# Two attention layers in one kernel: the first pair of the second layer scaled into other memory, its first biases added later, and the last two rows and the stored reciprocals handled in another order

## The chip, the cores and the metric

The kernel runs on one core of a Trainium2 chip. A core has TensorE (PE, with its weight loads shown apart as PEld), VectorE (DVE), ScalarE (ACT), GpSimd (POOL) and SyncE (SP), which here issues most DMAs. Each engine takes its instructions in the order in which the program wrote them, and waits on semaphores for what others produce. The metric is the device time of one execution in microseconds; lower is better.

## The reference

The input x has 128 rows of 256 positions with 256 channels. Two layers follow, each a residual attention over a group-normalised input:

```python
x = x + L0_conv_ref(_gn(x), ...)   # 8 heads, pair bias from z, mask, gate
x = x + L1_conv_ref(_gn(x), w_in, b_in, w_out, b_out, 16)

def L1_conv_ref(x, w_in, b_in, w_out, b_out, band):   # 4 heads, 64 channels each
    qkv = x @ w_in.T + b_in
    q, k, v = heads of the three thirds
    scores = q @ k.T / sqrt(64)
    keep = |i - j| <= band
    attn = softmax(where(keep, scores, -inf))
    return (attn @ v) @ w_out.T + b_out
```

The attention runs within a row of 256 positions. The group norm of layer 1 takes its means and variances over the whole output of layer 0, so layer 1 can't scale its first row before the last row of layer 0 is known.

## The kernel before, in words

All arithmetic is float32. Rows are handled in pairs: NP = 64 pairs of two rows. Layer 0 writes its output rows from the tile `xo` to a DRAM array `x1` (the trace calls it x), eight rows per store. Its weights wq, wk, wv and wg stay in tiles of 128 x 512 for the whole program.

**Between the layers.** The last pair's data for layer 1's pair 0 were loaded and turned early: they lie transposed in wq and wk. `norm1` works out a scale `R1c` and an offset `nM1` per channel, while TensorE runs products without use (L1882, called `busy`)[...]. `centre(k)` (L1948) then scales one half of a pair's transposed channels on ACT into the tile `xgT`, tag xgT, which has two buffers in a pool that lies where layer 0 had its tiles. Pair 0 is projected directly (`project`, `values`); from pair 1 on the projections use a scheme of seven products for eight (`product`, `join`), whose input differences `differences` computes on POOL. Pair 1 is loaded from `x1` by SP (L1930), transposed by DVE (`turn`, L1943) and scaled by ACT. `add_bias` (L1954) adds b_out on POOL to a pair's residual rows `xt`.

**The pair loop of layer 1** is written out by hand, one pass per pair p. `now` is pair p, `was` p-1, `old` p-2, `nxt` p+1, `nn` p+2, `n3` p+3. In each pass `now.scores` makes the scores of both rows, takes their exponentials on ACT and multiplies them by the band mask on POOL (L2063); `was.apply(1)` and `now.apply(0)` multiply by the values (L2077) and sum the weights (L2085); `nxt` is projected; `copy_sums`, `join_sums`, `invert` (L2108) and `weigh` (L2113) normalise; `was.out_product` makes the output projection; `old.keep_rows` adds the residual rows on POOL and stores.

**Range tests.** A kernel for general inputs stands behind this one. Whether it must run is decided at the end from the tile `ok`: `look` puts two entries on a queue, one reduction for the largest value, and a comparison with a reduction for the smallest (L2223, L2220, L2221, all on DVE). `some_checks(n)` takes n entries, from the queue `late` if it has any, else from `checks`. The reciprocals of the softmax sums of layer 1 are tested in two ways: those of the first 56 pairs are stored to the DRAM array `rsum1`, loaded again in pass 58 as one block of 128 x 896 and put on `checks`; those of the last LATE = 8 pairs are put on `late` straight from the tile. From pass 57 on a pass makes four late entries and takes four.

**The end.** After the loop come the rows of pair 62 (`out_row`), then those of pair 63: `out_block` makes the products on TensorE (L2133), all remaining entries run on DVE, `okmin` (L2389) is their least value, and `keep_row` (L2193) adds the residual on DVE and stores a row (L2201). A product with `ones` (L2394) counts the partitions that are in range, DVE writes `verdict` (L2396), every engine loads it, and branches (L2407) past the general kernel.

Of the kernel before, what the change touches and what calls it, by code (L numbers as in the profile page):

```python
# [9 lines left out]
F32 = mybir.dt.float32  # L10
AF = mybir.ActivationFunctionType
# [5 lines left out]
P = 128  # L17
# [756 lines left out]
def fast_kernel(  # L774
# [25 lines left out]
    nc = tc.nc  # L800
    S, I, C = x.shape
# [6 lines left out]
    NB = I // P  # L808
    KC = C // P
    NP = S // 2  # L810
    N2 = 2 * I
# [97 lines left out]
    def rows(ap, s0, n):  # L909
        return ap[s0 : s0 + n].rearrange("s (b p) c -> p (s b) c", p=P)  # L910
# [933 lines left out]
    LATE = 8  # L1844
    rsum1 = dram.tile([NP, H1, 2, I], F32, name="rsum1")
    with tc.tile_pool(name="l1", bufs=2) as sb, tc.tile_pool(
# [5 lines left out]
        def mm1(name, side=0):  # L1852
            return ps_s.tile([P, 512], F32, name=name, tag=f"s{side}")
# [67 lines left out]
        class Pair1:  # L1921
# [21 lines left out]
                nc.vector.transpose(self.xT.rearrange("p k n -> p (k n)"), self.xs.rearrange("p k n -> p (k n)"))  # L1943

            def centre(self, k):
                if k == 0:
                    self.xgT = sb.tile([P, KC, N2], F32, name="xgT1", tag="xgT")
                nc.scalar.activation(  # L1948
                    self.xgT[:, k, :], self.xT[:, k, :] if self.p else self.xT[k], AF.Identity,
                    bias=nM1[:, k : k + 1], scale=R1c[:, k : k + 1],  # L1950
                )

# [3 lines left out]
            def differences(self):  # L1956

                self.dT = sb.tile([P, 4, I], F32, name="dT1", tag="dT")
                b = [[self.xgT[:, k, r * I : (r + 1) * I] for r in range(2)] for k in range(KC)]
                t1, t2, t3, t4 = (self.dT[:, n] for n in range(4))  # L1960
                nc.gpsimd.tensor_tensor(t1, b[0][1], b[0][0], ALU.subtract)
                nc.gpsimd.tensor_tensor(t2, b[1][1], t1, ALU.subtract)
                nc.gpsimd.tensor_tensor(t3, b[1][1], b[0][1], ALU.subtract)
                nc.gpsimd.tensor_tensor(t4, b[1][0], t2, ALU.subtract)
# [10 lines left out]
            def product(self, n, i):  # L1975

                if len(self.ps) == n:
                    self.ps.append([mm1("ps_qk", n % 2) for _ in range(2)])
                    self.u.append(sm.tile([P, 3, I], F32, name="u1", tag=f"u{n}", bufs=1))
                x, y = (ps[:, :I] for ps in self.ps[n])  # L1980
                w = lambda m, k: w_in[:, k, n * C + m * P : n * C + (m + 1) * P]
                b = lambda k, r: self.xgT[:, k, r * I : (r + 1) * I]
                to, lhs, rhs, start = {
                    1: (x, w(0, 0), b(0, 0), True),
                    2: (y, w(0, 1), b(1, 0), True),
                    6: (x, wst[:, 1, n], self.dT[:, 1], False),
                    5: (y, wst[:, 0, n], self.dT[:, 0], True),
                    7: (x, wst[:, 2, n], self.dT[:, 2], False),
                    4: (x, w(1, 1), self.dT[:, 3], False),
                    3: (y, wst[:, 3, n], b(1, 1), False),  # L1990
                }[i]
                if n == 2:
                    for b in range(NB):
                        at = slice(b * P, (b + 1) * P)
                        nc.tensor.matmul(  # L1995
                            to[:, at], rhs[:, at], lhs, start=start and b == 0, stop=True, skip_group_check=True
                        )
                else:
                    nc.tensor.matmul(to, lhs, rhs, start=start, stop=True, skip_group_check=True)  # L1999
                u = self.u[n]  # L2000
                if i in (2, 5, 3):
                    return
                at = (1, 6, 7, 4).index(i)
                to = self.to[n](1, 0) if i == 4 else u[:, at]
                if n == 2:
                    nc.scalar.copy(to, x.rearrange("p (b c) -> p b c", b=NB) if i == 4 else x)
                else:
                    nc.scalar.activation(to, x, AF.Identity, bias=bin_c[:, n * KC + (at > 1) : n * KC + (at > 1) + 1])  # L2008
# [8 lines left out]
            def project(self, which, m):  # L2017
                n = ("qT", "kT").index(which)
                if m == 0:
                    setattr(self, which, sb.tile([P, KC, N2], F32, name=f"{which}1", tag=which))  # L2020
                ps = mm1("ps_p1", m)
                for k in range(KC):
                    nc.tensor.matmul(
                        ps, w_in[:, k, n * C + m * P : n * C + (m + 1) * P], self.xgT[:, k, :],
                        start=(k == 0), stop=(k == KC - 1),
                    )
                nc.scalar.activation(
                    getattr(self, which)[:, m, :], ps, AF.Identity, bias=bin_c[:, n * KC + m : n * KC + m + 1]
                )

            def values(self, r, side=0):
                if r == 0:
                    self.v = sb.tile([P, 2, NB, C], F32, name="v1", tag="v")
                ps = mm1("ps_v1", side)
                for b in range(NB):
                    t = r * NB + b
                    for k in range(KC):
                        nc.tensor.matmul(
                            ps[:, b * C : (b + 1) * C], self.xgT[:, k, t * P : (t + 1) * P], w_in[:, k, 2 * C : 3 * C],
                            start=(k == 0), stop=(k == KC - 1),  # L2040
                        )
                nc.scalar.copy(self.v[:, r, :, :].rearrange("p b c -> p (b c)"), ps)
# [142 lines left out]
            def keep_rows(self):  # L2185
                nc.gpsimd.tensor_tensor(self.yo, self.yo, self.xt, ALU.add)
                nc.sync.dma_start(rows(out, 2 * self.p, 2), self.yo)

            def keep_row(self, r):
                if r == 0:  # L2190
                    self.yo = sb.tile([P, 2 * NB, C], F32, name="yo", tag="yo")
                if self.p == NP - 1:
                    nc.vector.tensor_tensor(  # L2193
                        self.yo[:, r * NB : (r + 1) * NB, :], self.whole.rearrange("p (b c) -> p b c", b=NB),
                        self.xt[:, r * NB : (r + 1) * NB, :], ALU.add,
                    )
                for t in range(r * NB, (r + 1) * NB if self.p < NP - 1 else 0):
                    nc.vector.tensor_tensor(self.yo[:, t, :], self.y[t - r * NB], self.xt[:, t, :], ALU.add)
                s0 = 2 * self.p
                if self.p == NP - 1:  # L2200
                    nc.sync.dma_start(rows(out, s0 + r, 1), self.yo[:, r * NB : (r + 1) * NB, :])  # L2201
                elif r == 1:
                    nc.sync.dma_start(rows(out, s0, 2), self.yo)
# [34 lines left out]
        def load_sums(src, name):  # L2238
            t = sb.tile([P, src.shape[0] // P], F32, name=name, tag=name, bufs=1)
            nc.sync.dma_start(t, src.rearrange("(a b) -> a b", a=P))  # L2240
            look_all(t, 1e-16)

        with tc.manual_schedule():
# [9 lines left out]
            for m in range(KC):  # L2253
                now.project("qT", m)
                now.project("kT", m)
                nxt.centre(m)
            nxt.differences()
            for r in range(2):
                now.values(r)
            now.add_bias()  # L2260
            nxt.add_bias()
            look_all(eb.rearrange("p h b i -> p (h b i)"), math.exp(-20.0))
            n_eb = cols[0]

# [1 line left out]
            for p in range(NP - 1):  # L2266
# [4 lines left out]
                if p == 1:  # L2271
                    mask_t = sb.tile([S, I], F32, name="mask_all", bufs=1)
                    nc.sync.dma_start(mask_t, mask)
                    look_all(mask_t, 1e-15)
                    n_mask = cols[0]
                    load_sums(rsum.rearrange("n q r c i -> (n q r c i)"), "sums0")
                if p == NP - LATE + 2:
                    load_sums(rsum1[: NP - LATE].rearrange("n q r i -> (n q r i)"), "sums1")

                now.scores(0)  # L2280
                now.scores(1)
                old.keep_rows()
                was.apply(1)
                nxt.begin_fast()
# [92 lines left out]
            now.apply(1)  # L2377
            now.copy_sums(1)
            now.copy_odd(1)
            for b in range(NB):  # L2380
                now.out_block(0, b)
            now.join_sums(1)
            now.invert(1)
            now.join_odd(1)
# [2 lines left out]
            below(n_mask, cols[0], 1e8)  # L2387
            tot = sm.tile([P, 1], F32, name="okmin", bufs=1)
            nc.vector.tensor_reduce(tot, ok.rearrange("p a n -> p (a n)"), AX.X, ALU.min)  # L2389
            now.keep_row(0)  # L2390
            for b in range(NB):
                now.out_block(1, b)
            ps = mm1("ok_ps")
            nc.tensor.matmul(ps[:, 0:1], ones, tot, start=True, stop=True)  # L2394
            now.keep_row(1)
        nc.vector.tensor_scalar(verdict, ps[0:1, 0:1], P - 0.5, None, ALU.is_lt)  # L2396


# [63 lines left out]
```

## Time and profile before

| | |
|---|---|
| time, median of 3 runs | 3098.26 us (3097.44 to 3100.63) |
| time of the profiled execution | 3098.43 us |
| its span | 3096.7 us |
| mean granted TensorE clock | 0.987 |
| first scaling of layer 1 (L1948) | 1980.06 us |
| first pass that starts at the loop's usual distance (L2052) | 2026.3 us |
| start of the verdict (L2396) | 3089.94 us |

Lines of the timeline give the start, the duration, the engine, the source line, the operation, its output and inputs, and in brackets how long the engine had been idle and what released it. The chain of waits is followed back from the last instruction; its lines give the start, the length and what held the time. A line of the clock by stretches gives the stretch, its length, the busy time of PE, PEld, DVE, ACT and POOL with the number of instructions, the mean granted TensorE clock, the DMA share and GB/s.

### The profile page before, as it was taken

The page shows a single profiled execution, that of the slowest core. Times are in us where ns is not written, and L with a number is a line of the kernel's source. Part 1 is how long each engine was busy: PE and PEld are TensorE (multiplying, and loading weights), DVE is VectorE, ACT ScalarE, POOL GpSimd, SP SyncE. Part 2 cuts the span into 40 slices and gives each one's busy share as a digit, 9 for nine tenths or more (in the row PEclk, how much of TensorE's full clock was granted, in tenths as well). Part 3 has the DMA queues.
Part 4 walks back from the last instruction along what each step waited for, and adds up shares of the span by engine and source line. Part 5 has one row for each costly group of instructions (what it writes and reads, how often), then busy time and mean ns, then how long its engine had stood idle before and what let it go on. Part 6 is the DMA issues. An engine that isn't in the chain of part 4 may idle for free.

```text
span 3096.7 us, 83063 instructions
## 1 busy us (share of the span) xinstructions
PE 2991.3 (97%) x34386; PEld 2088.0 (67%) x34386; DVE 2374.1 (77%) x4075; ACT 1656.8 (54%) x2887; POOL 2587.0 (84%) x1950
## 2 busy tenths in 40 slices
PE   6689999999999999999999999899999999999998
PEld 4355555665555655555655555588888888888886
DVE  7987677777777777777777777688887877777787
ACT  3454544444444444444444444366666666666664
POOL 3469899898898888898888898588888888888885
PEclk9799999999999999999999999999999999999999
DMA  9952333323333332333333233433434343434341
GB/s 357 390 190 53 100 70 100 95 65 93 100 97 73 96 90 67 100 97 91 78 89 95 73 97 87 112 89 93 99 90 104 86 105 85 105 92 97 94 100 44
DMA packets 690787, 328.06 MB, mean 106 GB/s; under 512 B 538624, under 2 KB 639872, under 8 KB 689248
## 3 DMA queue, kind: packets, MB, share of 16 engines
q1 hardware_dynamic: 686000, 320.02, 38.8%
q8 instruction: 273, 4.47, 0.6%
q10 hardware_dynamic: 4400, 2.63, 0.3%
q14 instruction: 114, 0.93, 0.1%
HBM read 253.83 MB, written 68.74 MB: 104 GB/s over the span
## 4 chain that ended last, share of the span: by engine, by line
PE 89%; DVE 4%; DMA 4%; POOL 1%; issue 1%; ACT 1%; SPq 0%; ACTq 0%; POOLq 0%; DVEq 0%
PE ps_p L1364 21%; PE ps_qk L1999 12%; PE ps_sc L1401 9%; PE ps_ov L1436 8%; PE ps_v L1382 7%; PE ps_y L1490 7%; PE ps_su_y L2170 6%; PE ps_qk L1995 6%; PE ps_o L2077 4%; PE ps_su L1444 3%; PE ps_sc L2052 3%; PE ps_su_y L2085 2%; DMA xa<-in_x_dram 2%; DMA zt<-in_z_dram 1%; DVE st L1199 1%
## 5 line engine op out<-in xcount | busy, mean ns | idle before, releaser
L1425 POOL TENSOR_TENSOR eboth<-e 128x512 f32<-128x512 f32 x512 | 744.2, 1475 | 174.2 <-PE ps_su L1444 95.2
L1421 DVE TENSOR_TENSOR e<-ps_sc,eb 128x1024 f32<-128x1024 f32 x384 | 458.2, 1221 | 288.7 <-ACT ps_sc L1413 288.6
L1413 ACT ACTIVATE ps_sc<-ps_sc 128x1024 f32<-128x1024 f32 x384 | 375.4, 1007 | 435.8 <-PE ps_sc L1401 310.0
L2063 POOL TENSOR_TENSOR e<-e,bw 128x384 f32<-128x384 f32 x256 | 276.6, 1111 | 77.4 <-ACT e L2061 77.4
L1401 PE MATMUL ps_sc<-qT,kT 32*128 32x256 f32 x4096 | 293.9, 400 | 0.0
L1401 PEld LDWEIGHTS ps_sc<-qT,kT 32*128 32x128 f32 x4096 | 185.5, 184 | 101.5 <-issue 91.5
L1490 PEld LDWEIGHTS ps_y<-wo,oT 128*128 128x128 f32 x1024 | 194.2, 190 | 81.8 <-issue 44.0
L1436 PE MATMUL ps_ov<-e,v 128*32 128x256 f32 x4096 | 247.6, 382 | 1.1 <-DVE v L1388 1.1
L1364 PE MATMUL ps_p<-xnT,wq 128*128 128x512 f32 x512 | 247.5, 605 | 0.1
L1364 PE MATMUL ps_p<-xgT,wg 128*128 128x512 f32 x512 | 247.3, 605 | 0.0
L1490 PE MATMUL ps_y<-wo,oT 128*128 128x256 f32 x1024 | 242.0, 379 | 1.7 <-POOL oT L1480 1.7
L1382 PE MATMUL ps_v<-wv,xnT 128*128 128x256 f32 x1024 | 241.8, 379 | 0.0
L1364 PE MATMUL ps_p<-xnT,wk 128*128 128x512 f32 x512 | 240.7, 592 | 0.0
L1382 PEld LDWEIGHTS ps_v<-wv,xnT 128*128 128x128 f32 x1024 | 194.5, 190 | 54.0 <-issue 30.9
L2008 ACT ACTIVATE u<-ps_qk,bin_c 128x256 f32<-128x256 f32 x378 | 174.7, 477 | 93.0 <-PE ps_qk L1999 93.0
L2108 DVE RECIPROCAL rv<-sums 128x256 f32<-128x256 f32 x128 | 223.0, 1742 | 0.0
L1436 PEld LDWEIGHTS ps_ov<-e,v 128*32 128x32 f32 x4096 | 120.0, 109 | 109.4 <-issue 41.5
L1116 POOL TENSOR_TENSOR zrs<-zrs,mhalf 128x32 f32<-128x32 f32 (+1 forms) x19 | 87.9, 4631 | 114.4 <-DVE zrs L1109 114.4
L1371 ACT ACTIVATE gT<-ps_p,bg_c 128x512 f32<-128x512 f32 x128 | 87.9, 687 | 175.1 <-PE ps_p L1364 175.1
L1364 PEld LDWEIGHTS ps_p<-xnT,wk 128*128 128x128 f32 x512 | 97.2, 190 | 122.8 <-issue 122.6
L1999 PE MATMUL ps_qk<-dT,wst 128*128 128x256 f32 x756 | 173.5, 379 | 0.0
L1364 PEld LDWEIGHTS ps_p<-xnT,wq 128*128 128x128 f32 x512 | 91.9, 189 | 114.0 <-issue 112.0
(254 smaller groups left out, 7061.1 us busy)
## 6 DMA issues: line engine op xcount, KB each, us to landing
xa<-in_x_dram SPq DMA_DIRECT2D x8, 4096.0 KB
xt<-in_x_dram SPq DMA_DIRECT2D x64, 512.0 KB
x<-xo SPq DMA_DIRECT2D x16, 2048.0 KB
xt<-x SPq DMA_DIRECT2D x64, 512.0 KB
rvb<-rsum SPq DMA_DIRECT2D x252, 128.0 KB
xs<-x SPq DMA_DIRECT2D x252, 128.0 KB
out_dram<-yo SPq DMA_DIRECT2D x63, 512.0 KB
xs<-in_x_dram SPq DMA_DIRECT2D x248, 128.0 KB
```

The costliest lines, as they stand in the source:

```text
L1364: nc.tensor.matmul(ps, w[:, k, m * P : (m + 1) * P], getattr(self, src)[:, k, :], start=(k == 0), stop=(k == KC - 1),)
L1382: nc.tensor.matmul(self.ps_v[:, b * C : (b + 1) * C], self.xnT[:, k, t * P : (t + 1) * P], wv[:, k, :], start=(k == 0), stop=(k == KC - 1),)
L1401: nc.tensor.matmul(self.pss[q // 2][:, q % 2, b, :], self.kT[rs, c, r * I + b * P : r * I + (b + 1) * P], self.qT[rs, c, r * I : (r + 1) * I],
L1413: nc.scalar.activation(self.pss[a], ps, AF.Exp)
L1421: nc.vector.tensor_tensor(es[a], pss[a], eb[:, h : h + 2], ALU.mult)
L1425: nc.gpsimd.tensor_tensor(t, es[a][:, :, 0, :], es[a][:, :, 1, :], ALU.add)
L1436: nc.tensor.matmul(ov[q * D0 : (q + 1) * D0, c, :], self.v[:, r, b, h * D0 : (h + 1) * D0], es[q // 2][:, q % 2, b, :], start=(b == 0), st ...
L1490: nc.tensor.matmul(self.ps_y[:, b * C : (b + 1) * C], self.oT[r][:, k, b * P : (b + 1) * P], wo[:, k, :], start=(k == 0), stop=(k == KC - 1),)
L1995: nc.tensor.matmul(to[:, at], rhs[:, at], lhs, start=start and b == 0, stop=True, skip_group_check=True)
L1999: nc.tensor.matmul(to, lhs, rhs, start=start, stop=True, skip_group_check=True)
L2063: nc.gpsimd.tensor_tensor(e[:, q], e[:, q], bcast(bw.rearrange("p b w -> p (b w)"), 1, KC), ALU.mult)
L2108: nc.vector.reciprocal(self.rv[:, r, :], self.sums)
```

## The change

Four edits:

- `centre` puts pair 0's scaled input into wv and wg; the other pairs use the tile with the tag xgT as before. `xgT` becomes a list of two halves, and the methods that read it index the list. Pair 1's two scalings follow all of pair 0's projections instead of standing between them.
- The biases of pairs 0 and 1 are added in passes 0 and 1, behind the scores of both rows, instead of ahead of the loop.
- The stored reciprocals are loaded in two parts: those of the first 48 pairs in pass 50, those of the next 8 in pass 58.
- The last pair's residual rows go into PSUM by a product with the identity (`begin_row`), the output products accumulate on them, and ACT copies the sum and a store follows (`end_row`). `begin_row` of both rows and `end_row(0)` stand where `out_block(0, b)` stood, `end_row(1)` where `keep_row(0)` and `out_block(1, b)` stood.

```diff
             def centre(self, k):
-                if k == 0:
-                    self.xgT = sb.tile([P, KC, N2], F32, name="xgT1", tag="xgT")
+                if k == 0 and self.p:
+                    xgT = sb.tile([P, KC, N2], F32, name="xgT1", tag="xgT")
+                    self.xgT = [xgT[:, n, :] for n in range(KC)]
+                elif k == 0:
+                    self.xgT = [w.rearrange("p k c -> p (k c)") for w in (wv, wg)]
                 nc.scalar.activation(
-                    self.xgT[:, k, :], self.xT[:, k, :] if self.p else self.xT[k], AF.Identity,
+                    self.xgT[k], self.xT[:, k, :] if self.p else self.xT[k], AF.Identity,
                     bias=nM1[:, k : k + 1], scale=R1c[:, k : k + 1],
                 )
...
+            def begin_row(self, r):
+                if r == 0:
+                    self.yo = sb.tile([P, 2 * NB, C], F32, name="yo", tag="yo")
+                    self.last = []
+                ps = mm1("ps_y1", r)
+                self.last.append(ps)
+                for b in range(NB):
+                    nc.tensor.matmul(
+                        ps[:, b * C : (b + 1) * C], ident, self.xt[:, r * NB + b, :],
+                        start=b == 0, stop=False, skip_group_check=True,
+                    )
+            def end_row(self, r):
+                ps = self.last[r]
+                for b in range(NB):
+                    for k in range(KC):
+                        nc.tensor.matmul(
+                            ps[:, b * C : (b + 1) * C], self.oT[r][:, k, b * P : (b + 1) * P], w_out[:, k, :],
+                            start=False, stop=k == KC - 1, skip_group_check=True,
+                        )
+                t = self.yo[:, r * NB : (r + 1) * NB, :]
+                nc.scalar.copy(t, ps.rearrange("p (b c) -> p b c", b=NB))
+                nc.sync.dma_start(rows(out, 2 * self.p + r, 1), t)
...
             for m in range(KC):
                 now.project("qT", m)
                 now.project("kT", m)
+            for m in range(KC):
                 nxt.centre(m)
             nxt.differences()
             for r in range(2):
                 now.values(r)
-            now.add_bias()
-            nxt.add_bias()
...
+                if p == NP - 2 * LATE + 2:
+                    load_sums(rsum1[: NP - 2 * LATE].rearrange("n q r i -> (n q r i)"), "sums1")
                 if p == NP - LATE + 2:
-                    load_sums(rsum1[: NP - LATE].rearrange("n q r i -> (n q r i)"), "sums1")
+                    load_sums(rsum1[NP - 2 * LATE : NP - LATE].rearrange("n q r i -> (n q r i)"), "sums2")
                 now.scores(0)
                 now.scores(1)
+                if p < 2:
+                    now.add_bias()
...
             now.copy_odd(1)
-            for b in range(NB):
-                now.out_block(0, b)
+            for r in range(2):
+                now.begin_row(r)
+            now.end_row(0)
             now.join_sums(1)
             now.invert(1)
             now.join_odd(1)
...
             nc.vector.tensor_reduce(tot, ok.rearrange("p a n -> p (a n)"), AX.X, ALU.min)
-            now.keep_row(0)
-            for b in range(NB):
-                now.out_block(1, b)
+            now.end_row(1)
             ps = mm1("ok_ps")
             nc.tensor.matmul(ps[:, 0:1], ones, tot, start=True, stop=True)
-            now.keep_row(1)
```

More of the change, by code (lines that the diff above doesn't have):

```diff
@@ L1958, in differences @@
                 self.dT = sb.tile([P, 4, I], F32, name="dT1", tag="dT")
-                b = [[self.xgT[:, k, r * I : (r + 1) * I] for r in range(2)] for k in range(KC)]
+                b = [[self.xgT[k][:, r * I : (r + 1) * I] for r in range(2)] for k in range(KC)]
                 t1, t2, t3, t4 = (self.dT[:, n] for n in range(4))
@@ L1981, in product @@
                 w = lambda m, k: w_in[:, k, n * C + m * P : n * C + (m + 1) * P]
-                b = lambda k, r: self.xgT[:, k, r * I : (r + 1) * I]
+                b = lambda k, r: self.xgT[k][:, r * I : (r + 1) * I]
                 to, lhs, rhs, start = {
@@ L2023, in project @@
                     nc.tensor.matmul(
-                        ps, w_in[:, k, n * C + m * P : n * C + (m + 1) * P], self.xgT[:, k, :],
+                        ps, w_in[:, k, n * C + m * P : n * C + (m + 1) * P], self.xgT[k],
                         start=(k == 0), stop=(k == KC - 1),
@@ L2038, in values @@
                         nc.tensor.matmul(
-                            ps[:, b * C : (b + 1) * C], self.xgT[:, k, t * P : (t + 1) * P], w_in[:, k, 2 * C : 3 * C],
+                            ps[:, b * C : (b + 1) * C], self.xgT[k][:, t * P : (t + 1) * P], w_in[:, k, 2 * C : 3 * C],
                             start=(k == 0), stop=(k == KC - 1),
```

## The prediction

> **What bounds the kernel now.** I read the page's shares and its chain first, then the chain of waits in order of time at the layer boundary and at the end, then the timeline of both, then the clock by stretches.
>
> ```profile
> PE 2991.3 (97%) x34386; PEld 2088.0 (67%) x34386; DVE 2374.1 (77%) x4075; ACT 1656.8 (54%) x2887; POOL 2587.0 (84%) x1950
> PE 89%; DVE 4%; DMA 4%; POOL 1%; issue 1%; ACT 1%; SPq 0%; ACTq 0%; POOLq 0%; DVEq 0%
> ```
>
> TensorE is the path for 89% of the span. Time can be won only where it isn't: this change touches two such places. At the boundary the chain reads
>
> ```profile
> 1972.74 7.05 DMA x<-xo
> ...
> 1987.94 1.26 DVE xT L1943
> ...
> 1989.22 0.81 ACT xgT L1948
> ...
> 1994.13 4.63 POOL xt L1954 x2
> 1998.76 1.92 POOL e L2063 x2
> 2000.68 0.04 issue
> 2000.72 0.90 PE ps_o L2077 x50
> ```
>
> and the timeline there
>
> ```profile
> 1980.06 0.81 ACT L1948 ACTIVATE xgT<-wq,nM,R1c 128x512 f32<-128x512 f32 x1 [24.01 <-DMA x<-xo]
> 1991.79 1.06 ACT L2042 COPY v<-ps_v 128x512 f32<-128x512 f32 x2
> 1994.37 1.59 PEld L1999 LDWEIGHTS ps_qk<-xgT,w_in 128*128 128x128 f32 x8 [0.77 <-ACT e L2061]
> 2002.03 0.73 PEld L1999 LDWEIGHTS ps_qk<-dT,w_in 128*128 128x128 f32 x4 [0.30 <-issue]
> ```
>
> The reader should see that the two bias additions (4.63 us) stand ahead of pair 0's masks on POOL, so TensorE's first apply starts only when the masks arrive, and that pair 0's first scaling on ACT waits for the store of layer 0's last rows. From there to the tail TensorE is nearly gapless: passes of the pair loop take 16.74 us between their starts, some 17.0 to 18.4 with stalls that the chain calls issue. At the end:
>
> ```profile
> 3080.80 3.06 PEld L2133 LDWEIGHTS ps_y<-w_out,oT 128*128 128x128 f32 x8 [1.38 <-PE ps_su_y L2085]
> 3084.46 2.80 PEld L2133 LDWEIGHTS ps_y<-w_out,oT 128*128 128x128 f32 x8 [0.60 <-DVE oT L2113]
> ...
> 3088.58 0.25 DVE L2389 TENSOR_REDUCE okmin<-ok 128x1 f32<-128x96 f32 x1
> 3088.75 1.28 DVE L2193 TENSOR_TENSOR yo<-ps_y,xt 128x512 f32<-128x512 f32 x2
> ...
> 3089.94 0.14 DVE L2396 TENSOR_SCALAR verdict<-ok_ps 1x1 int32<-1x1 f32 x1
> ```
>
> and after it, on TensorE's queue,
>
> ```profile
> L2407 PEldq COMPARE_BRANCH  x1: 4510/4510/4510, 3091.0 to 3091.0; - x1
> ```
>
> DVE runs without a gap to the verdict; the branch on it (4.51 us on TensorE's queue) and the barrier close the span 6.76 us after the verdict's start. The stores, issued at 3089.45 and later, lie beside that branch. So the verdict's time sets the end. TensorE runs at half clock there:
>
> ```profile
> 3080.00:3084.00 4.00, 3.16 (x8) 2.52 (x8) 3.93 (x6) 0.69 (x2) 0.00 (x0) 0.51 0.00 0
> 3084.00:3087.00 3.00, 3.00 (x8) 2.09 (x7) 2.86 (x9) 0.00 (x0) 0.00 (x0) 0.51 0.00 0
> ```
>
> **What the skill says.** The Trainium skill, TensorE: Matmul & The Clock Gate, Part 1, has the clock halved after an idle window of about 3.4 us and restored after a busy one, the windows running freely. The trace agrees: by finer stretches it is halved from about 3080.13 to 3086.96, 6.83 us or twice 3.41, though TensorE worked 79% of the first window; and from about 1977.6 to 1981.0. DMA: Bandwidth & Descriptors, section Anatomy of one DMA, puts most of a transfer's fixed cost in the write receipt; here the last store of layer 0 lands at 1979.80 while its traffic fades at about 1979.1, so 0.7 us. SBUF — State Buffer, section on two separate sides, says that DVE operations with two SBUF inputs and POOL lock each other out of a shared port; L2113 took 1.06 us at 2010.60 beside POOL's masks against 0.68 alone. So moved POOL work can cost DVE 0.2 to 0.4 us.
>
> **Part A, the boundary.** *Free memory.* Pair 0's scaled input goes to wv and wg, last read by layer 0 before 1958, so the wait of L1948 for the store falls: it can start when nM1 ends, 1979.05, not 1980.06. TensorE gains less: its keep-warm products (four from 1977.40 in 3.57 us, at half clock) occupy it until about 1980.8, and the projections began at 1980.92. I count 0.1; were TensorE at full clock there, up to 1.0. *Order on ACT.* Pair 1's two scalings now follow all four projection copies. They wait for the transpose (1989.20), which is unchanged because it hangs on the same store and reload: 1989.22 to 1990.75 for two at 0.72 and 0.81. The value copies follow at once; the second waits for TensorE's values (1991.5) and ends at 1992.1, against 1992.85. TensorE's scores, row 0, start at 1991.47 as before, held by the values ahead of them. Row 1's start when the copies free their buffers, at 1992.2 rather than 1992.9. The exponentials take 0.44 each; row 0's start 0.94 after its scores (as 3063.87 to 3064.81), at 1992.41; row 1's first ends at 1993.75. That frees the buffer that L1999 waited for: 1993.85 instead of 1994.37, 0.5 won.
>
> *Biases behind the masks.* The 20 products of L1999 take 4.18 us of weight loads, then the usual 0.33: apply(0) can start at 1998.35. Its masks: POOL ends the differences at 1993.1 (from 1990.95, three at 0.7), then four masks at 0.97; row 0 is ready at 1995.0, row 1 at 1997.0. They no longer bind. From the start of apply to the next L1999 a pass takes 1.28 us (2033.61 to 2034.89), so 1999.6 against 2002.03: **2.4 us**. With full clock and the earlier projections I get 2.9, as ACT's scalings of pair 1 then bind. From below 1.9, if port locks take 0.5. Pair 0's bias (2.36 us) then runs at 1997.0 to 1999.4, before pair 2's scaled input exists (1999.7). Pair 1's runs in pass 1 behind its masks, in the 3.94 us that POOL idled before L2143. Nothing is queued behind either that is due sooner. The SP queue is not touched, and the third pair's reload has landed by then. I take 2.6, between clock states, because TensorE carries every later pass.
>
> **Part B, stored reciprocals.** A look is three DVE instructions, 0.98 us for 256 columns, 0.65 for 128. Before: 56 pairs, 896 columns, four looks loaded at pass 58, but from pass 57 the looks at live reciprocals have precedence, so all four ran after the loop. Now 48 pairs (768 columns) are loaded at pass 50 and looked at in passes 50 to 52, one look each, behind the last out_join, where passes 2 and 3 carry one in 16.74 us. Cost there: 0; if DVE is late, at most 1.0 in three passes. The load on SP (one issue, 0.47 us) goes behind the reload of pair 53, some 12 us ahead of its look. The last 8 pairs, one look of 128 columns, come after the loop in some_checks(6): 0.34 shorter than the look there now, which moves keep_row, the sums behind it and the whole tail by 0.34.
>
> **Part C, last residuals.** Per row TensorE adds two identity products (four instructions of 128x256, 0.217 us each at full clock): eight, 1.73 us, right after apply(1). Its weight loads end at 3079.42, less 0.34, so they run 3079.4 to 3081.1. Row 0's eight follow (to 3082.9), as its input is ready at 3080.4. Row 1 waits for DVE's L2113 (3084.41 less 0.34) and ends at 3085.9. ACT copies 0.59 and stores by 3087, beside the branch. DVE keeps three of its eight entries after L2113: the sums' entries from 3086.08 to 3088.37, 2.29 us, go. The additions of L2193 go too, 1.28, and with them their 0.6 before the verdict. So okmin runs 3085.95 to 3086.2, the ok_ps product ends at 3086.7, and the verdict starts at 3086.75 instead of 3089.94: **3.2 us**. At half clock TensorE binds: if it ends after one window kept busy, row 1 ends at 3086.2 and 3.0 remain; if two windows, as before, 1.6; if all 24 instructions run at 0.43, the verdict is at 3090 and nothing is won. I take 3.2, since the identity products fill the gap that left the first window unfilled.
>
> **Sum.** 2.6 + 3.2 = 5.8 us. The profiled execution took 3098.43 (span 3096.7 and 1.7 around it), so 3092.6; it lies 0.17 above the median of 3098.26, from which I get **3092.5**.
>
> **The rivals.** (1) *TensorE becomes the tail's bound at half clock*: for it, the 79% window that did not restore the clock; against it, the added work. 2.6 + 1.6 = 4.2: 3094.1. (2) *Full clock in both places and fewer stalls*: 2.9 + 3.2, and pass 1's stall of 0.75 ("issue" at 2010.77) gone, 6.9: 3091.4. For it: the windows run freely. Against it: the stalls come anywhere. (3) *Slower: the loop settles in another rhythm.* With POOL's order changed in passes 0 and 1, masks reach TensorE late in every pass. Price: per pass what they are late; at 0.2 us, 61 passes give 12, less 5.8: 3104.7. It decides from 0.1 us a pass. For it: passes 57 to 62 take 17.1 because DVE's look falls in mid-pass. Against it: POOL idles about 2.5 us a pass and catches up. (4) The stored-reciprocal look waits for its load: needs 12 us of delay, counted within (3).
>
> **How the numbers follow.** Forecast 0.66, (1) 0.10, (2) 0.18, (3) 0.06. Some 55 passes hold about 16 us of scattered stalls of 0.3 to 1.7; moved code can shift their sum by 2 us, and the three runs before spread over 3.2. The limit of what a measurement of this kernel can tell is 0.2%, 6.2 us, just beyond my 5.8: the forecast case falls half on each side (0.32 beyond), (2) nearly all beyond (0.16). So faster 0.48, same 0.46, slower 0.06. Range 3089.8 to 3096.0: the forecast with 2.5 to 3.5 on either side, (1) and (2) in it; (3) is left out.
>
> **What would show it.** Right: L1948's first at about 1979.1; L1999 at 1993.8; POOL's L1954 behind L2063; no wait at the first L2077; looks at sums at passes 50 to 52; 3 entries after the last L2113; the verdict's start 5.5 to 6 us earlier. Wrong: passes longer than 16.74 without issue, ok_ps waiting for row 1's products instead of okmin, or a later landing of pair 1's reload.

## The result and the profile after

The changed kernel takes 3092.81 us (median of 20 runs, 3090.59 to 3096.82) against 3098.72 us before (20 runs, 3095.52 to 3100.78): 5.9 us less, a ratio of 0.9981 with a 95% interval of 0.9974 to 0.9987. The gain is clear of zero and lies just inside the 0.2% that the prediction took as its limit. The profiled execution took 3093.70 us, its span is 3092.0.

The page's shares and its chain by engine, changed kernel:

```profile
PE 2985.4 (97%) x34394; PEld 2086.2 (67%) x34394; DVE 2373.0 (77%) x4073; ACT 1658.4 (54%) x2889; POOL 2585.2 (84%) x1950
PE 89%; DMA 4%; DVE 3%; POOL 1%; issue 1%; ACT 1%; SPq 0%; ACTq 0%; POOLq 0%; DVEq 0%
```

TensorE has eight more matmuls and DVE two instructions fewer; the shares can't show where 5.9 us went. The chain of waits at the boundary does (start, length, what held the time):

```profile
1972.29 7.07 DMA x<-xo
...
1987.37 1.26 DVE xT L1943
1988.63 0.02 issue
1988.65 1.52 ACT xgT L1951 x2
1990.17 0.96 ACT v L2045 x2
1991.13 0.04 issue
1991.18 0.94 PE ps_sc L2055 x30
1992.12 0.48 ACT e L2064
1992.60 0.04 issue
1992.65 4.58 PE ps_qk L2002 x20
1997.23 0.86 PE ps_o L2080 x54
```

POOL's biases and masks are gone from it. After the reload (up to 1987.37) come pair 1's scalings, the value copies, the second row's scores and exponential, and from 1992.65 on TensorE without a break. The timeline of the same place:

```profile
1978.68 0.81 ACT L1951 ACTIVATE wv<-wq,nM,R1c 128x512 f32<-128x512 f32 x1 [23.08 <-DVE nM L1898]
1996.24 2.37 POOL L1957 TENSOR_TENSOR xt<-xt,bout_r 128x1024 f32<-128x1024 f32 x1
1997.16 0.76 PEld L2080 LDWEIGHTS ps_o<-e,v 64*32 64x32 f32 x63 [0.33 <-issue]
1998.48 0.73 PEld L2002 LDWEIGHTS ps_qk<-dT,w_in 128*128 128x128 f32 x4 [0.30 <-ACT xgT L1951]
```

The first scaling is released by nM1 and no longer by the store; pair 0's bias stands alone behind the masks; the first apply has only the usual 0.33 us ahead of it. At the end the timeline reads

```profile
3077.76 2.87 PEld L2200 LDWEIGHTS ps_y<-xt,ident 128*128 128x128 f32 x8 [0.30 <-issue]
3080.71 3.78 PEld L2210 LDWEIGHTS ps_y<-w_out,oT 128*128 128x128 f32 x16
3084.20 0.25 DVE L2422 TENSOR_REDUCE okmin<-ok 128x1 f32<-128x96 f32 x1
3084.57 0.35 PEld L2425 LDWEIGHTS ok_ps<-okmin,ones 128*128 128x128 f32 x2
3085.05 0.15 DVE L2426 TENSOR_SCALAR verdict<-ok_ps 1x1 int32<-1x1 f32 x1 [0.59 <-PE ok_ps L2425]
```

and the clock by stretches (stretch, length, busy us of PE, PEld, DVE, ACT and POOL with counts, granted TensorE clock, DMA share, GB/s)

```profile
3078.00:3080.00 2.00, 2.00 (x6) 1.55 (x6) 1.94 (x4) 0.73 (x2) 0.00 (x0) 0.50 0.04 8
3080.00:3082.00 2.00, 2.00 (x8) 1.65 (x7) 1.97 (x3) 0.00 (x0) 0.00 (x0) 0.65 0.00 0
3082.00:3084.00 2.00, 2.00 (x11) 1.77 (x10) 1.93 (x7) 0.59 (x1) 0.00 (x0) 1.00 0.00 0
```

TensorE was at half clock again as the identity products began, but this stretch lasted 3.41 us (3078.00 to 3081.41), half as long as the 6.83 us before.

For everything below two stretches are read from each profile. **A** runs from the start of nM1 (L1898) to the start of pass 1's scores; **E** from the start of the scores of the last pair's second row to the start of the verdict (the expectation of the first experiment calls them the last pair's first scores; 19.74 us before the verdict at 3089.94 lies 3070.20, where the second row's scores start). Between the two profiled executions the time divides so: up to nM1 0.47 us less (layer 0, where nothing was changed), A 29.49 to 26.41 (3.08 less), the stretch between A and E 1061.82 to 1063.73 (1.91 more), E 19.74 to 16.49 (3.25 less), and 0.17 more after the verdict: 4.7 together. Most of the 1.91 are stalls: of passes 1 to 56, 33 take 16.74 or 16.75 us before and after, and the others hold 16.3 us of stalls before and 18.0 after. In the ten profiles below this sum lies between 14.2 and 18.5 us, with the boundary's edits and without them, so 1.91 is within its scatter.

### The profile page after: what moved, and what is told of

It is laid out like the page before. It is cut to its first block, busy times and chain, and to the rows that moved or that the text cites. A ratio compares the mean times of both kernels' runs of the same rounds, so it can differ in the third digit from the quotient of the medians.

```text
span 3092.0 us, 83079 instructions
## 1 busy us (share of the span) xinstructions
PE 2985.4 (97%) x34394; PEld 2086.2 (67%) x34394; DVE 2373.0 (77%) x4073; ACT 1658.4 (54%) x2889; POOL 2585.2 (84%) x1950
## 4 chain that ended last, share of the span: by engine, by line
PE 89%; DMA 4%; DVE 3%; POOL 1%; issue 1%; ACT 1%; SPq 0%; ACTq 0%; POOLq 0%; DVEq 0%
PE ps_p L1364 21%; PE ps_qk L2002 12%; PE ps_sc L1401 9%; PE ps_ov L1436 8%; PE ps_v L1382 7%; PE ps_y L1490 7%; PE ps_su_y L2173 6%; PE ps_qk L1998 6%; PE ps_o L2080 4%; PE ps_su L1444 3%; PE ps_sc L2055 3%; PE ps_su_y L2088 2%; DMA zt<-in_z_dram 2%; DMA xa<-in_x_dram 1%; DVE st L1199 1%
```

## The experiments

Ten kernels, 12 to 21 runs each. The medians stand beside those of the kernel before on the same chip. E repeats within 0.1 us from profile to profile; A spreads over 0.8 us in the profiles that have the same edits, for reasons that are taken apart below. A ratio's interval here is about 1.5 thousandths wide (4 to 5 us), so the parts are read from the profiles and the times only bear them out.

| kernel | median us | before, us | ratio and 95% interval | A | E |
|---|---|---|---|---|---|
| boundary alone | 3094.34 | 3097.02 | 0.9992, 0.9984 to 1.0 | 26.07 | 19.74 |
| end alone | 3094.02 | 3097.02 | 0.9989, 0.9982 to 0.9996 | 29.34 | 16.44 |
| sums alone | 3094.87 | 3097.02 | 0.9991, 0.9983 to 1.0 | 28.76 | 17.31 |
| rows alone | 3097.09 | 3097.02 | 1.0001, 0.9992 to 1.0009 | 28.64 | 19.17 |
| memory back | 3092.31 | 3096.70 | 0.9988, 0.9979 to 0.9996 | 27.00 | 16.43 |
| biases back | 3093.54 | 3096.70 | 0.9990, 0.9984 to 0.9997 | 27.48 | 16.42 |
| order back | 3092.46 | 3096.70 | 0.9986, 0.9979 to 0.9992 | 27.56 | 16.42 |
| late looks at the end | 3098.07 | 3096.70 | 1.0004, 0.9995 to 1.0012 | 26.04 | 16.43 |
| three late pairs | 3092.46 | 3097.81 | 0.9983, 0.9976 to 0.9989 | 26.81 | 16.63 |
| same, identity early | 3091.09 | 3097.81 | 0.9979, 0.9972 to 0.9985 | 26.04 | 16.64 |

### The two halves of the change

Boundary alone: the changed kernel with one load of stored reciprocals and the old end.

```diff
-                if p == NP - 2 * LATE + 2:
-                    load_sums(rsum1[: NP - 2 * LATE].rearrange("n q r i -> (n q r i)"), "sums1")
                 if p == NP - LATE + 2:
-                    load_sums(rsum1[NP - 2 * LATE : NP - LATE].rearrange("n q r i -> (n q r i)"), "sums2")
+                    load_sums(rsum1[: NP - LATE].rearrange("n q r i -> (n q r i)"), "sums1")
...
-            for r in range(2):
-                now.begin_row(r)
-            now.end_row(0)
+            for b in range(NB):
+                now.out_block(0, b)
...
-            now.end_row(1)
+            now.keep_row(0)
+            for b in range(NB):
+                now.out_block(1, b)
...
+            now.keep_row(1)
```

> The boundary's edits alone (pair 0 in wv and wg, pair 1's scalings behind the projections, biases of pairs 0 and 1 behind the masks); end and stored reciprocals as before. Stretch A runs from the start of nM1 (L1898) to the start of pass 1's scores: 29.49 us before, 26.41 in the changed kernel. Stretch E runs from the start of the last pair's first scores to the start of the verdict: 19.74 before, 16.49 changed. Theory, two local and independent gains: A 26.4 (full clock) to 27.0 (half clock), E 19.7, the time about 3 us under the kernel before. Rival, the loop settles in another rhythm and gives it back: A short, but passes longer than 16.74 us without a stall and no gain in the time.

A was 26.07 and E 19.74; the time fell by 2.7 us, with an interval of 0 to 5.0. No pass rhythm gave it back: 35 of the passes 1 to 56 took 16.74 or 16.75 us.

End alone: the changed kernel with the three boundary edits undone (their diffs stand below).

> Stored reciprocals in two parts and the residual rows through TensorE, the boundary as before. Theory: A 29.5, E 16.5 to 16.8, the time 3.2 us under the kernel before. Rival, TensorE at half clock becomes the bound of the end: E 18.1 and the ok_ps product waits for row 1's products, not for okmin. Second rival, the load in pass 50 costs its passes something: pass 50 to 52 longer than before by 1 us or more.

A was 29.34 and E 16.44, the end at full clock, with 3.0 us less. Each half leaves the other's stretch as it was (E 19.74 with the boundary alone, A 29.34 with the end alone), so the two are independent; the times, 2.7 + 3.0 = 5.7 of the 5.9 us, fit this, but with their intervals they couldn't show it. The look in pass 50 runs at its end (in the changed kernel at 2859.70, 23 us after its load was issued at 2836.96). Passes 50 to 52 took 18.68, 16.74 and 17.24 us in the changed kernel and 18.68, 16.75 and 16.75 with the end alone, against 18.41, 16.74 and 17.23 before, so neither load nor looks can be seen in them.

### The end's two edits apart

Sums alone: as "end alone", with `out_block` and `keep_row` in place of `begin_row` and `end_row`.

> Stored reciprocals in two parts alone; residuals added by DVE as before. If the end is DVE's alone, E falls by the entries, 2.29 + 0.34, to 17.1. If TensorE's products of row 1 at half clock bind the additions of L2193 once the entries are gone, E is 17.8 at half clock and 17.2 at full clock.

Rows alone: as "end alone", with the stored reciprocals in one load.

> Residual rows through TensorE alone; the stored reciprocals in one block as before. Theory: DVE's entries still run to okmin, only the 0.55 us that the verdict waited behind the additions of L2193 go: E 19.2. Rival, the additions were the larger part: E 17.5 to 18.5.

E fell by 2.43 with the sums alone (17.31) and by 0.57 with the rows alone (19.17): together 3.00 of the 3.25 to 3.30 that both give. The timeline of "sums alone" shows what the rest is:

```profile
3085.49 0.25 DVE L2418 TENSOR_REDUCE okmin<-ok 128x1 f32<-128x96 f32 x1
3085.66 0.68 DVE L2220 TENSOR_TENSOR yo<-ps_y,xt 128x512 f32<-128x512 f32 x1
3086.55 0.69 DVE L2220 TENSOR_TENSOR yo<-ps_y,xt 128x512 f32<-128x512 f32 x1 [0.21 <-PE ps_y L2134]
3087.15 0.14 DVE L2425 TENSOR_SCALAR verdict<-ok_ps 1x1 int32<-1x1 f32 x1
```

With fewer entries okmin comes early, but the verdict stands behind both additions, and the second waited 0.21 us for TensorE's row 1, which ran at half clock until 3085.30. The value is between the two that were expected for full and half clock and above 17.1: DVE was not alone there, but nearly. In "rows alone" okmin is at 3085.89 and the verdict follows 0.79 later, as it does wherever the additions are gone (0.85 in the changed kernel), where it followed 1.36 later before. So the looks were most of the end's gain, and the new rows took the additions out of the verdict's way.

### The boundary's three edits, undone one at a time

Memory back:

```diff
-                if k == 0 and self.p:
+                if k == 0:
                     xgT = sb.tile([P, KC, N2], F32, name="xgT1", tag="xgT")
                     self.xgT = [xgT[:, n, :] for n in range(KC)]
-                elif k == 0:
-                    self.xgT = [w.rearrange("p k c -> p (k c)") for w in (wv, wg)]
```

> The changed kernel with pair 0's scaled input back in the tile with the tag xgT. Stretch A (start of nM1 to the start of pass 1's scores) is 26.41 in the changed kernel's profile, which ran at full clock there. Theory: the first scaling waits for the store again, about 1 us longer than nM1 needs; at full clock TensorE's projections and values shift by 0.9 and the products by 0.7 to 0.9, A 27.1 to 27.3; at half clock 0.1 to 0.3 (A up to 27.0). Rival, memory is worth nothing because pair 1's reload binds: A 26.4 at full clock.

Biases back:

```diff
             for r in range(2):
                 now.values(r)
+            now.add_bias()
+            nxt.add_bias()
...
-                if p < 2:
-                    now.add_bias()
```

> The changed kernel with both bias additions ahead of the loop again. Theory: POOL's masks of row 0 are ready about 1.9 us after TensorE wants them, A 28.2. Rival, the products start early enough for POOL not to matter or another wait takes its place: A under 27.

Order back:

```diff
                 now.project("kT", m)
-            for m in range(KC):
                 nxt.centre(m)
```

> The changed kernel with pair 1's scalings between the projections again. Theory: two projection copies and the value copies wait behind the transpose on ACT, row 1's scores and the products start 0.5 (half clock) to 1.1 us (full clock) later, A 26.9 to 27.5. Rival, the order costs nothing since the scores wait for the values anyway: A 26.4.

A was 27.00, 27.48 and 27.56, against 26.04 to 26.81 in the five profiles that have all three edits. The spread of the five is as wide as what an edit is worth, so A is divided further. All times in this table are read from the profiles and counted from the start of nM1, but the last column, which is A less the one before it; "half" means that TensorE was at half clock in the 3.4 us up to the start of the projections, or to within 0.15 us of it:

| kernel | clock | projections | pair 1's transpose | its first product | from there to pass 1's scores |
|---|---|---|---|---|---|
| before | half | 2.03 | 9.05 | 15.48 | 14.01 |
| end alone | half | 2.00 | 8.96 | 15.39 | 13.95 |
| sums alone | full | 2.06 | 8.37 | 14.83 | 13.93 |
| rows alone | full | 2.03 | 8.24 | 14.80 | 13.84 |
| changed | full | 1.12 | 8.95 | 14.23 | 12.18 |
| boundary alone | full | 1.13 | 8.14 | 13.90 | 12.17 |
| late looks at the end | full | 1.13 | 8.46 | 13.89 | 12.15 |
| three late pairs | half | 2.00 | 8.58 | 14.66 | 12.15 |
| same, identity early | full | 1.12 | 8.25 | 13.89 | 12.15 |
| memory back | full | 2.09 | 8.43 | 14.85 | 12.15 |
| biases back | full | 1.12 | 8.20 | 13.89 | 13.59 |
| order back | full | 1.12 | 8.99 | 15.41 | 12.15 |

The first product starts at the later of two times. One is 12.77 us after the start of the projections, wherever the clock was full and pair 1's reload from `x1` was early. The other hangs on the transpose: 6.42 us after it in the old order (before, end alone, order back), 5.28 in the new one (changed). With "order back", 8.99 + 5.28 would have been 14.27, so the order is worth 1.14 where the reload is late; with the earliest one, 8.14, the same sums give 14.56 and 13.89, so an estimated 0.67. With "memory back", 1.12 + 12.77 would have been 13.89, so the memory is worth 0.96 at full clock where the reload is early; at half clock nothing, as the projections then start at 2.00 with it (three late pairs) as without it. The products without use (L1882) run in every one of these kernels, and the clock was halved beside them from about 1977 on in three of the twelve profiles; no run leaves them out. The biases are worth 1.44 to 1.86 (13.59 to 14.01 against 12.15): no kernel with the memory or the order back shows any of it.

The waits are the ones that were named. With the memory back, from its timeline:

```profile
1979.69 0.81 ACT L1949 ACTIVATE xgT<-wq,nM,R1c 128x512 f32<-128x512 f32 x1 [24.05 <-DMA x<-xo]
1980.56 7.13 PE L2024 MATMUL ps_p<-xgT,w_in 128*128 128x512 f32 x16 [1.61 <-ACT xgT L1949]
```

TensorE stood 1.61 us before its projections, against 0.65 in the changed kernel's profile, and the whole row behind them came later. With the biases back:

```profile
1991.88 4.68 POOL L1957 TENSOR_TENSOR xt<-xt,bout_r 128x1024 f32<-128x1024 f32 x2
1996.50 3.89 POOL L2066 TENSOR_TENSOR e<-e,bw 128x384 f32<-128x384 f32 x4
1998.52 0.73 PEld L2080 LDWEIGHTS ps_o<-e,v 64*32 64x32 f32 x59 [0.82 <-POOL e L2066]
```

The apply waits for its mask again. It cost 1.44 us, less than the 1.8 that the expected 28.2 stands for, as pair 1's reload came early in that execution, and with it POOL's differences, behind which the biases and the masks stand. With the order back:

```profile
1989.41 0.81 ACT L1951 ACTIVATE xgT<-xT,nM,R1c 128x512 f32<-128x512 f32 x1 [4.72 <-DVE xT L1943]
1990.70 0.67 ACT L2030 ACTIVATE kT<-ps_p,bin_c 128x512 f32<-128x512 f32 x1
1991.42 0.69 PEld L2055 LDWEIGHTS ps_sc<-qT,kT 64*64 64x64 f32 x30 [0.39 <-ACT kT L2030]
```

ACT idled 4.72 us before the transpose while a finished projection waited for its copy, and the scores waited for that copy.

### Trying for more

Late looks at the end of the pass:

```diff
                 was.row_sums()
-                some_checks(2 if p > NP - LATE else 0)
...
-                some_checks(2 if p > 0 else 0)
+                some_checks((4 if p > NP - LATE else 2) if p > 0 else 0)
```

> The changed kernel with the looks at live reciprocals of passes 57 to 62 moved: both of a pass at its end instead of one in its middle. Theory: the middle one lies on DVE's chain between two products' operands (0.37 us a pass over 16.74), at the end there is room: passes 58 to 62 at 16.75 and about 2 us won. Rival: two looks at the end (2 us) hold back the next reciprocal, passes of 17.0 or more and nothing won.

The theory fell. The last passes of the loop and the stretch behind it, to the scores of the last pair's second row, took 114.40 us against 108.02 in the changed kernel; four passes of 18.1 us stand in its trace, and its time, 1.4 us above the kernel before, shows nothing of the other edits' gain. The timeline of one:

```profile
3011.06 0.28 DVE L2249 TENSOR_SCALAR above<-rv 128x256 f32<-128x256 f32 x1
3011.72 0.41 DVE L2252 TENSOR_REDUCE ok<-rv 128x1 f32<-128x256 f32 x1
3012.04 0.91 DVE L2249 TENSOR_SCALAR above<-rv 128x256 f32<-128x256 f32 x1
3013.32 1.74 DVE L2111 RECIPROCAL rv<-sums 128x256 f32<-128x256 f32 x1
3016.20 0.41 DVE L2105 TENSOR_TENSOR sums<-ps_su_y,sums 128x256 f32<-128x256 f32 x1
```

One look is hidden at the end of a pass, the second is not: it delays the reciprocal, behind it the join of the sums and the first joins of the products, for which TensorE waits (1.49 us at 3017.00 in this pass). Its comparison, moreover, took 0.91 us beside POOL's masks, where the first took 0.28.

Three late pairs: fewer pairs are looked at live, so that fewer passes carry a middle look.

```diff
-    LATE = 8
+    LATE = 3
+    EARLY = 48
...
-                if p == NP - 2 * LATE + 2:
-                    load_sums(rsum1[: NP - 2 * LATE].rearrange("n q r i -> (n q r i)"), "sums1")
-                if p == NP - LATE + 2:
-                    load_sums(rsum1[NP - 2 * LATE : NP - LATE].rearrange("n q r i -> (n q r i)"), "sums2")
+                if p == EARLY + 2:
+                    load_sums(rsum1[:EARLY].rearrange("n q r i -> (n q r i)"), "sums1")
+                if p == NP - 2:
+                    load_sums(rsum1[EARLY : NP - LATE].rearrange("n q r i -> (n q r i)"), "sums2")
```

> The changed kernel with LATE = 3: the reciprocals of pairs 48 to 60 are stored and loaded in pass 62 as one block of 208 columns, so that passes 57 to 61 carry no look at live reciprocals. Theory: each of these five passes falls from 17.11 to 16.75 (apart from stalls), 1.8 us less from pass 56 to the end; stretch E gains 0.1 to 0.2 for the larger block, 16.6. Rival: what makes these passes long isn't the look but the end of the loop (fewer pairs left, other transfers), and they stay at 17.1.

Passes 58 to 61 fell from 17.11, 17.34, 17.11 and 17.11 us to 16.75 each: the look made them long. Pass 57 kept 17.34 (17.45 in the changed kernel), with a stall of 0.38 us that the trace calls issue. Pass 62, now the only one with a middle look, takes longer (22.55 us from its scores to E against 21.90; why wasn't tried), so 1.15 us remain of the expected 1.8; E is 16.63. The time, 5.35 us under the kernel before, can't be told from the changed kernel's 5.9.

The same with the identity products ahead of the last apply:

```diff
             some_checks(1)
+            for r in range(2):
+                now.begin_row(r)
             now.apply(1)
...
-            for r in range(2):
-                now.begin_row(r)
             now.end_row(0)
```

> The kernel with LATE = 3 and, besides, the identity products of both rows ahead of the last apply, in TensorE's 2.2 us gap. If DVE's chain to okmin sets stretch E, E stays where it is with LATE = 3 alone (16.6). If TensorE's products of the rows set it, E falls by up to 1.7.

E was 16.64, the same to a hundredth, though TensorE now waits 2.13 us for DVE before row 1, against 1.42 with LATE = 3 alone:

```profile
3080.87 1.59 PEld L2211 LDWEIGHTS ps_y<-w_out,oT 128*128 128x128 f32 x8 [2.13 <-DVE oT L2117]
3082.58 0.25 DVE L2423 TENSOR_REDUCE okmin<-ok 128x1 f32<-128x96 f32 x1
```

So at full clock, at which both profiles ran there, DVE's chain sets the end; behind row 1 TensorE stands another 0.48 us, in both, before the ok_ps product. Neither tests the end at half clock. This kernel has the lowest median of all, 3091.09, 6.7 us under the kernel before; its interval, 0.9972 to 0.9985, overlaps that of the changed kernel, so that it is better isn't shown.

## Why the prediction was right

**The time.** Predicted 3092.5, measured 3092.8; predicted 5.8 us of gain, measured 5.9. The gain came from the places and through the waits that it named. That the numbers agree to 0.3 us is in part luck: the interval of the gain, 4.0 to 8.1 us, can't tell so much. The sign that the verdict would start 5.5 to 6 us earlier failed in the profiled pair, 4.9, for the stalls between A and E.

**Part A, predicted 2.6 (2.4 at half clock, 2.9 at full).** Between the two profiles it was 3.08: 1.25 up to the first product and 1.83 behind it, where the prediction had 0.5 ("0.5 won") and 1.9. But the profile before had the half clock ahead of its projections and the changed kernel's had not. Like with like, the gain is 2.5 to 2.7 at half clock (29.34 and 29.49 against 26.81) and 2.6 to 2.7 at full clock with the reload as early (28.64 and 28.76 against 26.04 to 26.07). So the first forecast was a little low and the second a little high, and 2.6 between them came out right. All waits went as described: L1948 by nM1, the masks ahead of the biases, pair 1's bias in the gap of pass 1. The free memory was sized right in both states of the clock (0.1 at half and up to 1.0 at full; measured 0.0 and 0.96). The order on ACT was argued too narrowly: 0.5 was reckoned from a later copy of the values, with TensorE's scores "held by the values ahead of them". At half clock they are (row 0's scores start 12.41 us after nM1 with the edits, 12.52 and 12.58 without), and the first product came 0.7 to 0.8 earlier. With the memory freed and full clock the values end sooner; "order back" shows the copy of pair 0's last projection held behind the transpose, and the scores held by that copy, which is up to 1.14. What the prediction held fixed and is not fixed is the landing of pair 1's reload: the transpose starts 8.1 to 9.1 us after nM1.

**Part B, predicted nothing in the loop, 2.29 + 0.34 at the end.** Passes 50 to 52 show nothing. The sums alone gave 2.43, the rest (0.2) being TensorE's row 1 behind which the additions waited.

**Part C, predicted 0.6 of the end's 3.2.** The rows alone gave 0.57. Both together gave 3.25 to 3.30. The half clock fell on the end in five of the twelve profiles. With the old rows (before, boundary alone, sums alone) it lasted 6.83 us, and TensorE was busy for 79 to 82% of the first 3.41; with the identity products (changed, biases back) TensorE was busy for all of the first 3.41, and it lasted no longer. So the forecast that the identity products fill the window and end it after one was right. Here the Trainium skill, TensorE: Matmul & The Clock Gate, Part 1, was borne out in that a busy window brings the clock back. Its idle window isn't what these traces show ahead of the halving: TensorE was busy for 39% of the last 3.41 us before it in the kernel before and for 47% in the changed one. The half clock cost E 0.07 at most (16.49 in the changed kernel and 16.42 with the biases back, against 16.42 to 16.44 at full clock), less than the 0.2 that the prediction gave one window, but it used up TensorE's room: the idle time ahead of the ok_ps product is 0.48 us at full clock, 0.16 with the biases back and 0.08 in the changed kernel, whose verdict comes 0.06 later behind okmin. There DVE and TensorE end about level.

**The rivals.** TensorE as the bound of the end came close but cost no more than 0.07 us; two windows of half clock with the new rows didn't occur and stay untested. The other rhythm didn't come: passes without a stall are 16.74 before and after. The stalls that the prediction gave 2 us of scatter took 1.9 in the profiled pair, to the worse; the times of the 20 runs can't show them apart. That the gain would fall about as likely above as below 6.2 us was fair: 5.9, with an interval of 4.0 to 8.1 us.

## What to carry to other kernels

Where an in-order queue stands at a boundary between stages, ask of each instruction what else is due behind it: work that nobody waits for yet (biases) behind work that the next engine wants (masks), and a copy that is ready ahead of one that waits for a transfer. A tile may wait for memory and not for data: the first write of a stage into memory that the last stage is still storing from waits for that store, and a tile that died earlier saves the wait; here that was worth 0.96 us where TensorE stood ready, and nothing where it was busy until then. At the end of a program follow what the last decision hangs on; work can move from the engine that carries that chain to one that idles, but count what room that engine has: here 0.48 us at full clock, and next to none after a window of half clock.

## What was not expected

A DVE comparison of 128x256 from SBUF to SBUF took 0.28 us alone, 0.77 in the middle looks, beside POOL's differences of the rows, and 0.73 to 0.91 beside POOL's masks. In all twelve profiles each such comparison that began while a POOL instruction ran ended 0.15 us after that instruction, whether 0.15 or 0.77 us of it were left, so it waited for it. The prediction had cited the Trainium skill (SBUF — State Buffer, on two separate sides) for operations with two inputs; its section on who interferes with whom adds that a tensor_scalar, which this comparison is, can enter a mode in which it shares POOL's ports and one of the two waits. The trace agrees. A middle look makes its pass 0.37 us longer, two looks at the end 1.4 us; how much of that is this wait (0.49 and 0.63 us of DVE's time) and how much the look itself wasn't tried apart.

The stalls that the chain calls issue come at the same passes in different kernels: the pass that ends at 2503.84 before and the one that ends at 2500.39 after both took 18.11 us, and from pass 8 to pass 50 a long pass of 17.5 to 18.7 returns every seventh pass in both (the last three end at 2623.44, 2742.30 and 2861.17 before, at 2619.99, 2739.39 and 2859.32 after). In all twelve profiles passes 15, 22, 29, 36, 43 and 50 take 17.6 to 19.0 us, and 1.3 to 2.1 us after the longest stall in each the queue that the page lists as q8, instruction, starts a packet of 16 KB. This is only a hint: what they wait for wasn't tried; that they go with the place in the program and not with the data or the time is only what the pattern suggests.
